# Layer 1 of a four-layer kernel: background pieces in two parts, linked convolution groups, and a preparation that waits for PSUM

## Chip, cores and metric

The kernel runs on one core of one Trainium2 chip, in float32 throughout. The metric is the device time of one execution in microseconds (us). A core has TensorE (PE, matrix multiplies into PSUM), VectorE (DVE), ScalarE (ACT), GpSimd (POOL), and DMA queues; the SyncE queue (SP) issues most loads. Each engine executes its own list of instructions in the order in which the program issues them.

## What is computed

The input is 8 images of 64 channels by 64 x 64 positions, and four layers follow each other. The change concerns layer 1 alone, a state space layer with a gated feed-forward part. Cut to what matters:

```python
xn = ln(x);  xm, z = split(xn @ in_proj)          # 64 -> 2 x 128 channels
u  = silu(conv3x3_depthwise(xm))                  # 128 channels, 4096 positions
for way in range(4):                              # rows, columns, and both backwards
    dt, B, C = project(u)                         # dt = softplus(...), 16 states
    h[n] = exp(dt * A[n]) * h[n] + dt * B[n] * u  # a scan over 4096 positions
    y += sum over n of h[n] * C[n]   (+ D * u)
x1 = x + out_proj(ln(y) * silu(z))
a, b = split(conv3x3_depthwise(conv1x1(ln(x1))))  # 2 x 170 channels
out = x1 + conv1x1(gelu(a) * b)
```

## The kernel before

**Steps and slots.** Layer 1 (function `layer1`) cuts each image's scan into 16 steps: four ways times four pieces of T = 1024 positions, so 8 images give 128 steps. A step is 16 slots, one for each of the 16 states. The function `stream` (which layers 2 and 3 use too) issues the slots one after another. In slot i it issues:

- SP: loads of B for state i+5 and of C for state i+3, each spread from one row to 128 partitions;
- POOL: `multiply_b(i+2)` (L465), hb = du * B, into one of three buffers;
- DVE: `scan(i)` (L481), which turns the decay dA and hb into h;
- DVE or POOL: `multiply_c(i)` (L495), h * C. In slots 1, 4, 7, 10 and 13 ("shared") POOL does it, in the next slot, and h gets a tile of its own in SBUF. In the other 11 slots DVE does it, and h overwrites the decay in PSUM;
- ACT: `keep` (L1211), one column of h for the next piece, and `decay(i+2)` (L472), the exponential for two slots later. The decays have two PSUM tiles;
- PE: `gather(i-2)`, which adds hc to the sum of the step in PSUM through the identity matrix (L287, four matrix passes). The first gather of a step stands in slot 2, and there the sum of the step before is drained (L1226 on ACT for the first way of an image, L1228 on DVE for the others).

**Background work.** Two kinds of work are threaded through the slots as Python generators (`Task`). One is `prepare` of the next step: a projection (L287 into `mm`), a copy to `dbl` (L1184), two small transfers (L1187), the matmul for dt (L1191), then softplus (L396) and du (L1198). The other is a queue named `behind` with, for each image, `finish` (norm of y, output projection), `begin` (norm, convolution and z of the image after the next) and `feed` (the feed-forward part). Inside them `statistics` computes means of squares (Square L907, mean L912, copy L917, small transfer L918, square root L922, reciprocal L924), `place` writes a normed tile into a padded image (ACT L895, POOL L896), `group` is one convolution group of 6 full-height (L879) and 6 half-height (L887) matmuls, and `gated` has three groups in each of four chunks (gelu L1091 and L1102, products L1094 and L1105). `finish` multiplies the norm by z on POOL (L1023) and then by the centred y on DVE (L1028).

**What sets the order.** All background work shares one PSUM tile, `mm`. A generator says at each `yield` what its next piece needs: True means that it holds `mm` and must go on before another may use it (`stream` keeps it in `held`), False that its next piece needs no PSUM, None that it is about to take `mm`, and CALM that it holds `mm` but goes on only in slots where neither this nor the next state is shared. In each slot `stream` advances the preparation by one piece and the background by one piece. A piece is issued before the slot's scan, and, where slot i-2 was shared, before its gather (`late`); after the scan come `multiply_c` and `decay(i+2)`. At slot 2 of each step (`start = 2`) the next preparation starts, and because it needs `mm`, this loop first issues everything that is held, at once:

```python
while self.held or self.urgent:
    self.advance(behind)
work = Task(steps[at + 1].prepare())
```

After the last slot `rest` finishes the last image's `finish` and `feed` with a second PSUM tile.

Of the kernel before, what the change touches and what calls it, by code (L numbers as in the profile page):

```python
# [13 lines left out]
PSUM = bass.MemoryType.PSUM  # L14
# [8 lines left out]
T = 1024  # L23
# [188 lines left out]
    return ap.rearrange("p (a b) -> p a b", b=ref.shape[2])  # L212


CALM, CALM_FREE = "calm", "calm, no PSUM"


class Task:

    def __init__(self, pieces):
        self.pieces, self.said, self.calm, self.over = pieces, None, False, False

    def step(self):
        try:
            self.said = next(self.pieces)
        except StopIteration:
            self.said, self.over = False, True  # L230
        self.calm = self.said in (CALM, CALM_FREE)
        if self.calm:
            self.said = self.said == CALM

# [15 lines left out]
class Net:  # L250
# [147 lines left out]
    def advance(self, behind, room=True, calm=True):  # L398


        while True:
# [9 lines left out]
                return  # L411
            queue.popleft()

    def stream(self, pools, ahead, steps, behind, rest=None):

# [49 lines left out]
        def decay(i):  # L467
            if i < total:
                s, n = steps[i // NS], i % NS
                dA[i] = pe.tile([128, T], F32, name="dA")  # L470
                for cut, A in s.lanes:
                    nc.scalar.activation(dA[i][:, cut], s.dt[:, cut], AF.Exp, scale=A[:, n : n + 1])  # L472
# [13 lines left out]
        def calm(i):  # L486

            return i + 1 >= total or not (shared(i) or shared(i + 1))
# [27 lines left out]
            multiply_b(i)  # L516
        for i in range(2):
            decay(i)
        work, self.held, self.urgent = None, None, deque()
        for i in range(total + 2):  # L520
            at, n = divmod(i, NS)
            need(i + ahead[0], "bc")
            need(i + ahead[1], "du")
            fetch(i + ahead[0])
            fetch_c(i + ahead[2])
            multiply_b(i + ahead[1])
            if 0 < i <= total and shared(i - 1):
                multiply_c(i - 1)


            first = i > NS and n == 2
            late = i > 1 and not first and steps[0].late and shared(i - 2)
            if i > 1 and not late and not first:
                gather(i - 2)
            if at + 1 < len(steps) and n == steps[at].start:
                steps[at + 1].ready()
                while self.held or self.urgent:
                    self.advance(behind)
                work = Task(steps[at + 1].prepare())
            if work is not None and not (self.held and work.said is None) and (calm(i) or not work.calm):  # L540
                work.step()
                if work.over:
                    work = None
            room = work is None or work.said is not True and (n < steps[0].early or hasattr(steps[at + 1], "du"))
            self.advance(behind, room, calm(i))
            if late:
                gather(i - 2)
            if i < total:
                scan(i)
            if first:  # L550
                gather(i - 2)
            if i < total:
                if not shared(i):
                    multiply_c(i)
            decay(i + 2)
        steps[-1].drain(acc.pop(len(steps) - 1))
        steps[-1].done()
        while self.held:
# [262 lines left out]
    def layer1(self, src, dst):  # L821
        nc, tc, d = self.nc, self.tc, self.d
        mid = self.hbm["x1a"]
        with ExitStack() as ctx:
# [65 lines left out]

            def place(rows, normed, g, b):

                yield False
                o = rows[:C, :, 1 : 1 + HW]
                nc.scalar.activation(o, like(normed[:C], o), AF.Identity, bias=b[:C], scale=g[:C])  # L895
                nc.gpsimd.tensor_copy(rows[C:, :, 2 : 2 + HW], o)  # L896

            def statistics(hold, centred, halves, eps, chunks=range(4)):

                rs = p1.tile([128, 32], F32, name="rs")
                for c in chunks:
                    ps = yield from centred(c)
                    sq = tp.tile([128, T], F32, name="tmp")
                    nc.scalar.activation(sq, ps, AF.Square)  # L907
                    ps = pp.tile([128, T], F32, name="mm")
                    if halves:
                        for r in range(2):  # L910
                            at, o = slice(r * C, r * C + C), slice(r * 512, r * 512 + 512)
                            nc.tensor.matmul(ps[:1, o], mean[at, 0:1], sq[at, o], start=True, stop=True)  # L912
                    else:
                        self.mm(ps[:1], mean[:, 1:2], sq)
                    yield True
                    ms = tp.tile([1, T], F32, name="tmp")
                    nc.scalar.copy(ms, ps[:1])  # L917
                    nc.scalar.dma_start(rs[c * 32 : c * 32 + 32, :], ms.rearrange("o (p e) -> o p e", e=32))  # L918
                yield False
                yield False  # L920
                rs = rs[chunks[0] * 32 : chunks[-1] * 32 + 32]
                nc.scalar.activation(rs, rs, AF.Sqrt, bias=eps[: len(chunks) * 32])  # L922
                yield False
                nc.vector.reciprocal(rs, rs)  # L924
                yield False
                if chunks[0] == 0:
                    hold["rs"] = h1.tile([1, L], F32, name="rs")
                row = hold["rs"][:, chunks[0] * T : chunks[-1] * T + T]
                nc.sync.dma_start(row.rearrange("o (p e) -> (o p) e", e=32), rs)
                yield False  # L930
                yield False
# [6 lines left out]
            def begin(b):  # L938
# [15 lines left out]
                n = (HW + 2) * (HW + 2)  # L954
# [19 lines left out]
                    yield from place(pad[0][:, 1 + c * 16 : 17 + c * 16], inv, g1, b1)  # L974
                hold["u"] = p2.tile([128, L], F32, name="u")
                for c in range(4):
                    yield
                    ps = pp.tile([128, T], F32, name="mm")
                    for half in range(2):
                        conv_half(ps, taps, slice(0, 128), pad, c * 16, half)  # L980
                        yield True
                    conv_right(ps, taps, slice(0, 128), pad, c * 16)
                    yield True
                    yield True
                    nc.scalar.activation(hold["u"][:, c * T : c * T + T], ps, AF.Silu, bias=cb)
                for c in range(4):
                    yield
                    ps = pp.tile([128, T], F32, name="mm")
                    for r in range(2):
                        at, f = slice(r * C, r * C + C), 1 + c * 16 + r * 8  # L990
                        o = ps[:, r * 512 : r * 512 + 512].rearrange("p (a b) -> p a b", b=HW)
                        nc.tensor.matmul(
                            o, w_z[at], pad[0][at, f : f + 8, 1 + r : 1 + r + HW], start=True, stop=True
                        )
                    yield True
                    z = tp.tile([128, T], F32, name="tmp")
                    nc.scalar.activation(z, ps, AF.Silu)  # L997
                    nc.scalar.dma_start(hz[b, :, c * T : c * T + T], z)
# [51 lines left out]
            def feed(b, part=None):  # L1050
# [37 lines left out]
                def gated(c):  # L1088
                    ps = yield from group(c, slice(0, 128))
                    g = tp.tile([128, T], F32, name="tmp")  # L1090
                    nc.scalar.activation(g, ps, AF.Gelu)  # L1091
                    yield
                    ps = yield from group(c, slice(128, 256))
                    nc.vector.tensor_tensor(g, ps, g, ALU.mult)  # L1094
                    yield
                    x = tokens(mid, b, c)
                    ps = yield from group(c, slice(256, 362))

# [4 lines left out]
                    yield True  # L1103
                    yield True
                    nc.vector.tensor_tensor(h[:42], ps[C : C + 42], h[:42], ALU.mult)  # L1105
                    yield
                    ps = pp.tile([128, T], F32, name="mm")
                    self.mm(ps[:C], pout[:, 0, :], g, start=True, stop=False)
                    yield True
# [32 lines left out]
            behind = deque()  # L1142
# [19 lines left out]
            ways = (1, 3, 2, 0)  # L1162

            class Step:
                start, early, late = 2, 8, True
                shared = (1, 4, 7, 10, 13)
                shaped = staticmethod(lambda t: t)

# [8 lines left out]
                def prepare(self):  # L1177
# [7 lines left out]
                    self.bc = hp.tile([NS, 2, T], F32, name="bc")  # L1185
                    for m in range(2):
                        nc.scalar.dma_start(self.bc[:, m, :], dbl[4 + m * NS : 4 + m * NS + NS])  # L1187
                    pt = pp.tile([128, T], F32, name="mm")
                    for r in range(2):
                        at, o = slice(r * C, r * C + 4), slice(r * 512, r * 512 + 512)  # L1190
# [55 lines left out]
            with tc.manual_schedule():  # L1246
# [4 lines left out]
                steps = [Step(b, k, j) for b in range(NB) for k in ways for j in range(4)]  # L1251
# [227 lines left out]
    def l2_scan(self, hx, hy):  # L1479
        nc, tc, d = self.nc, self.tc, self.d  # L1480
        with ExitStack() as ctx:
# [34 lines left out]
            carries = {}  # L1516

            class Step:
                bc_shape, start, early, late = [128, 2, T], 1, 0, False
                shared = (1, 4, 7, 10, 13)  # L1520
                rev = False
                shaped = staticmethod(lambda t: t)
# [220 lines left out]
    def l3_stage(self, s, src, dst):  # L1743
# [5 lines left out]
        W, H = 512, 512 // HW  # L1749
        with ExitStack() as ctx:  # L1750
# [103 lines left out]
            behind = deque()  # L1854
# [1 line left out]
            images = {}  # L1856

            class Step:
                bc_shape, start, early, late = [128, 2, W], 1, 0, False
                first = staticmethod(lambda n: 0.0)  # L1860
                keep = staticmethod(lambda n, h: None)
                shaped = staticmethod(lambda t: t.rearrange("p (j t) -> p j t", j=2))
# [155 lines left out]
```

## Time and profile before

| | us |
|---|---|
| median of 3 runs (25488.44 to 25513.53) | 25492.16 |
| the profiled execution, its own time | 25501.22 |
| its span, first to last instruction | 25499.4 |
| layer 1's slots, first scan to last scan (1337 to 8673) | 7336 |
| a step of layer 1 without background work (4020.0 to 4072.1) | 52.1 |
| a step with convolution groups (3786.0 to 3846.3) | 60.3 |

The slots of layer 1 are 29% of the span. A step's length is read as the distance between the scans of its first slot and of the next step's first slot. The sum over the whole span, where DVE is busy 88% and POOL 86%, is an average over four layers; the steps of layer 1 are where the change acts, and in them the two lengths of the table differ by the time that background work adds.

### The profile page before, as it was taken

The numbers are of one execution on the slowest core, as the hardware profiler recorded it, in microseconds if no ns is written. First come the engines' busy times: TensorE is split into PE (matmuls) and PEld (weight loads), VectorE is DVE, ScalarE is ACT, GpSimd is POOL, SyncE is SP. The second block draws the span as 40 slices with busy tenths as digits, with TensorE's granted clock in tenths as the row PEclk, the third lists the DMA queues.
The fourth block names the chain that finished last, engine by engine and source line by source line (L and its number), as shares of the span: only waits on it lengthen the run. The fifth ranks groups of instructions, "written<-read, shape, count | busy, mean of one in ns | idle before, by whom it ended". The sixth has DMA issues, their size and how long they took to land. (4 is left out here: it accounts for less than half of the span.)

```text
span 25499.4 us, 193264 instructions
## 1 busy us (share of the span) xinstructions
PE 21439.3 (84%) x53146; PEld 8356.0 (33%) x53146; DVE 22515.7 (88%) x13020; ACT 14749.0 (58%) x18562; POOL 22003.6 (86%) x10679
## 2 busy tenths in 40 slices
PE   8777888888888888877888888888878888888888
PEld 5522333333333323322333333333333333333333
DVE  4379989999889679965999999999989999999999
ACT  4345555555555455512666666666666666666666
POOL 0089999999999669953999999999989999999999
PEclk9888999999999999988999999999989999999999
DMA  2289899898888668821555555555545555555554
GB/s 60 80 285 319 312 315 315 309 316 314 308 312 313 209 237 323 325 77 37 168 170 169 170 168 170 169 169 167 168 155 169 169 169 167 171 167 170 168 171 157
DMA packets 1772399, 5282.72 MB, mean 207 GB/s; under 512 B 536352, under 2 KB 542564, under 8 KB 1703472
## 3 DMA queue, kind: packets, MB, share of 16 engines
q1 hardware_dynamic: 1744176, 5207.00, 60.2%
q10 hardware_dynamic: 27136, 63.34, 0.8%
q8 instruction: 423, 6.93, 0.1%
q14 instruction: 664, 5.44, 0.1%
HBM read 5112.85 MB, written 156.11 MB: 207 GB/s over the span
## 5 line engine op out<-in xcount | busy, mean ns | idle before, releaser
L465 POOL TENSOR_TENSOR hb<-du,bc 128x1024 f32<-128x1024 f32 x4608 | 10746.9, 2356 | 495.0 <-DVE h L481 329.6
L287 PE MATMUL acc<-hc,ident 128*128 128x512 f32 x18816 | 8893.4, 614 | 87.3 <-DVE img L1228 56.7
L472 ACT ACTIVATE dA<-dt,w_A 128x512 f32<-128x512 f32 x8192 | 5662.7, 691 | 4115.1 <-DVE hc L495 3127.9
L481 DVE TENSOR_TENSOR_SCAN dA<-dA,hb 128x1024 f32<-128x1024 f32 x3384 | 7725.9, 2283 | 283.0 <-ACT dA L472 109.0
L287 PE MATMUL acc<-h,ident 128*128 128x512 f32 x7808 | 4552.5, 713 | 2373.9 <-POOL h L495 2373.7
L287 PEld LDWEIGHTS acc<-hc,ident 128*128 128x128 f32 x18816 | 3695.6, 200 | 5299.5 <-issue 4672.2
L465 POOL TENSOR_TENSOR hb<-du,b 128x1024 f32<-128x1024 f32 x2048 | 4880.6, 2415 | 489.4 <-DVE h L481 255.6
L495 DVE TENSOR_TENSOR hc<-dA,bc 128x1024 f32<-128x1024 f32 x3296 | 4034.5, 1224 | 261.1 <-issue 8.9
L472 ACT ACTIVATE dA<-dt,w_l_A 128x1024 f32<-128x1024 f32 x2560 | 2856.5, 1117 | 1183.2 <-DVE hc L495 757.6
L481 DVE TENSOR_TENSOR_SCAN dA<-dA,carry,hb 128x1024 f32<-128x1024 f32 x1320 | 3094.5, 2344 | 169.7 <-ACT carry L1211 109.1
L287 PEld LDWEIGHTS acc<-h,ident 128*128 128x128 f32 x7808 | 1544.6, 215 | 5032.0 <-POOL h L495 3170.5
L481 DVE TENSOR_TENSOR_SCAN h<-dA,hb 128x1024 f32<-128x1024 f32 x1352 | 3082.0, 2280 | 48.1 <-ACT dA L472 43.0
L495 POOL TENSOR_TENSOR h<-h,bc 128x1024 f32<-128x1024 f32 x1312 | 3088.9, 2354 | 14.2 <-DVE h L481 14.2
L495 DVE TENSOR_TENSOR hc<-dA,c 128x1024 f32<-128x1024 f32 x1408 | 1723.2, 1224 | 118.0 <-DMA c<-bc 6.5
L495 POOL TENSOR_TENSOR h<-h,c 128x1024 f32<-128x1024 f32 x640 | 1519.1, 2374 | 7.5 <-ACT carry L1211 7.1
L481 DVE TENSOR_TENSOR_SCAN h<-dA,carry,hb 128x1024 f32<-128x1024 f32 x600 | 1404.7, 2341 | 82.4 <-ACT dA L472 79.2
L472 ACT ACT_TABLE_LOAD x1122 | 1439.5, 1283 | 21.3 <-ACT tmp L997 1.2
L1211 ACT COPY carry<-dA 128x1 f32<-128x1 f32 x1056 | 167.8, 159 | 1725.3 <-DVE hc L495 1662.7
L1885 PE MATMUL mm<-xn,taps 128*128 128x512 f32 x2048 | 937.7, 600 | 33.5 <-POOL xn L1851 31.3
L694 POOL MEMSET xf<- 128x24 f32 x33 | 4.3, 141 | 910.6 <-PE ps L715 701.9
L339 POOL COPY strip<-plain 64x1024 f32<-64x1024 f32 x256 | 266.3, 1040 | 462.2 <-ACT plain L1612 454.1
L1900 PE MATMUL mm<-u,w_xp 128*36 128x512 f32 x1024 | 516.6, 629 | 140.8 <-ACT u L1897 136.3
(310 smaller groups left out, 19000.0 us busy)
## 6 DMA issues: line engine op xcount, KB each, us to landing
bc<-bc SPq DMA_DIRECT2D x4096, 512.0 KB
b<-bc SPq DMA_DIRECT2D x2048, 512.0 KB
c<-bc SPq DMA_DIRECT2D x2048, 512.0 KB
bc<-bc SPq DMA_DIRECT2D x512, 1024.0 KB
tmp<-rs SPq DMA_DIRECT2D x93, 512.0 KB
raw<-x SPq DMA_DIRECT2D x64, 512.0 KB
inv<-rs SPq DMA_DIRECT2D x64, 512.0 KB
tmp<-x SPq DMA_DIRECT2D x192, 128.0 KB
```

What stands on the lines that cost most here:

```text
L287: self.nc.tensor.matmul(o, lhsT, r, start=start, stop=stop)
L339: self.nc.gpsimd.tensor_copy(pair[e][0][r * C : r * C + C, rows, 1 + r : 1 + r + HW], v)
L465: nc.gpsimd.tensor_tensor(s.shaped(hb[i]), s.shaped(s.du), B.pop(i), ALU.mult)
L472: nc.scalar.activation(dA[i][:, cut], s.dt[:, cut], AF.Exp, scale=A[:, n : n + 1])
L481: nc.vector.tensor_tensor_scan(h[:, way], dA[i][:, way], hb.pop(i)[:, way], s.first(n), ALU.mult, ALU.add)
L495: engine.tensor_tensor(s.shaped(o), s.shaped(h), CC.pop(i), ALU.mult)
L694: nc.gpsimd.memset(x[:, :, HW:], 0.0)
L1211: nc.scalar.copy(self.carry[:, n : n + 1], h[:, last : last + 1])
L1885: nc.tensor.matmul(tokens(px[:, j * W : j * W + W]), taps[k][:, m, j * 128 : j * 128 + 128], xn[:, :, f : f + HW], start=m == 0, stop=m == 1,)
L1900: nc.tensor.matmul(pd, xp[:, k, j, :], u[:, j * W : j * W + W], start=j == 0, stop=j == 1)
```

## The change

A piece may now come in two parts. A generator that says MID has its next piece issued in the same slot, after the slot's gather, scan, product and decay: the new function `complete`, called at the end of each slot, steps the preparation and the held task while they say MID. MID stands in `place` (before ACT and POOL write the tile), in `statistics` (before the mean), and in `prepare` (before the matmul for dt).

LINK stands where one convolution group, one z chunk or one gated product ends and the next begins. It is read as MID, so that the next group's first matmuls are issued in the same slot, unless a preparation is waiting for PSUM or is due in the next slot (`Task.wanted`); then it is read as None, as before.

A preparation that is due at slot 2 is now `pending`. It starts when nothing is held, and only from slot 2 + `patience` (4) on does it issue the held work at once. While it waits, no new background task takes `mm`. Layers 2 and 3 have `patience = 0`, no MID and no LINK. `statistics` says False once more before its square root.

```diff
-CALM, CALM_FREE = "calm", "calm, no PSUM"
+CALM, CALM_FREE, MID, LINK = "calm", "calm, no PSUM", "in two parts", "in two parts, or two pieces"
...
 class Task:
+    wanted = False
...
-        self.pieces, self.said, self.calm, self.over = pieces, None, False, False
+        self.pieces, self.said, self.calm, self.over, self.mid = pieces, None, False, False, False
...
-        self.calm = self.said in (CALM, CALM_FREE)
+        if self.said == LINK:
+            self.said = None if Task.wanted else MID
+        self.calm, self.mid = self.said in (CALM, CALM_FREE), self.said == MID
+        if self.mid:
+            self.said = True
...
+    def complete(self, work):
+        for task in (work, self.held[0] if self.held else None):
+            while task is not None and task.mid:
+                task.step()
+        if self.held and self.held[0].said is not True:
+            if self.held[0].over:
+                self.held.popleft()
+            self.held = None
...
             if at + 1 < len(steps) and n == steps[at].start:
                 steps[at + 1].ready()
+                pending = True
+
+            if pending and (n >= steps[at].start + steps[at].patience or not (self.held or self.urgent)):
                 while self.held or self.urgent:
                     self.advance(behind)
-                work = Task(steps[at + 1].prepare())
+                work, pending = Task(steps[at + 1].prepare()), False
...
+            Task.wanted = pending or n == steps[0].start - 1
             room = work is None or work.said is not True and (n < steps[0].early or hasattr(steps[at + 1], "du"))
-            self.advance(behind, room, calm(i))
+            self.advance(behind, room and not (pending and not (self.held or self.urgent)), calm(i))
...
             decay(i + 2)
+            self.complete(work)
...
@@ place
-                yield False
+                yield MID
                 o = rows[:C, :, 1 : 1 + HW]
                 nc.scalar.activation(o, like(normed[:C], o), AF.Identity, bias=b[:C], scale=g[:C])
...
@@ statistics
                     nc.scalar.activation(sq, ps, AF.Square)
+                    yield MID
                     ps = pp.tile([128, T], F32, name="mm")
...
+                yield False
                 yield False
                 yield False
                 rs = rs[chunks[0] * 32 : chunks[-1] * 32 + 32]
...
@@ begin
-                    yield
+                    yield LINK if c else None
                     ps = pp.tile([128, T], F32, name="mm")
...
-                    yield
+                    yield LINK
                     ps = pp.tile([128, T], F32, name="mm")
...
@@ gated (at three places)
-                    yield
+                    yield LINK
...
@@ Step
-                start, early, late = 2, 8, True
+                start, early, late, patience = 2, 8, True, 4
...
                         nc.scalar.dma_start(self.bc[:, m, :], dbl[4 + m * NS : 4 + m * NS + NS])
+                    yield MID
                     pt = pp.tile([128, T], F32, name="mm")
```

More of the change, by code (lines that the diff above doesn't have):

```diff
@@ L518, in stream @@
             decay(i)
-        work, self.held, self.urgent = None, None, deque()
+        work, pending, self.held, self.urgent = None, False, None, deque()
         for i in range(total + 2):
@@ L1091, in gated @@
                     nc.scalar.activation(g, ps, AF.Gelu)
-                    yield
+                    yield LINK
                     ps = yield from group(c, slice(128, 256))
                     nc.vector.tensor_tensor(g, ps, g, ALU.mult)
-                    yield
+                    yield LINK
                     x = tokens(mid, b, c)
@@ L1105, in gated @@
                     nc.vector.tensor_tensor(h[:42], ps[C : C + 42], h[:42], ALU.mult)
-                    yield
+                    yield LINK
                     ps = pp.tile([128, T], F32, name="mm")
@@ L1518, in l2_scan @@
             class Step:
-                bc_shape, start, early, late = [128, 2, T], 1, 0, False
+                bc_shape, start, early, late, patience = [128, 2, T], 1, 0, False, 0
                 shared = (1, 4, 7, 10, 13)
@@ L1858, in l3_stage @@
             class Step:
-                bc_shape, start, early, late = [128, 2, W], 1, 0, False
+                bc_shape, start, early, late, patience = [128, 2, W], 1, 0, False, 0
                 first = staticmethod(lambda n: 0.0)
```

## The prediction

> **What bounds the kernel now.** I read the busy time by stages first, for two steps of layer 1: one without background work, one with convolution groups (columns: window, length, then busy us of PE, PEld, DVE, ACT, POOL, then clock, DMA share, GB/s).
>
> ```profile
> 4020.01:4072.13 52.12, 38.13 (x73) 14.43 (x72) 50.71 (x29) 22.68 (x21) 50.10 (x23) 0.87 0.92 309
> 3785.96:3846.27 60.31, 53.66 (x137) 20.05 (x136) 53.18 (x31) 30.73 (x28) 51.63 (x23) 1.00 0.85 295
> ```
>
> In the first DVE and POOL are both full: 52.1 us is the floor of a step. In the second DVE works 2.5 us more, yet the step lasts 8.2 us more, so DVE stands still. Next, who DVE waits for in all of layer 1 (total us, times, longest):
>
> ```profile
> DVE dA L481 <- ACT carry L1211: 176.2, 133, 3.1
> ...
> DVE tmp L1105 <- ACT tmp L1102: 69.7, 13, 5.4
> DVE tmp L1028 <- POOL tmp L1023: 62.4, 27, 4.3
> DVE dA L481 <- ACT dA L472: 58.0, 47, 3.6
> DVE tmp L1094 <- PE mm L887: 56.3, 28, 6.6
> DVE h L481 <- ACT dA L472: 56.2, 30, 4.5
> ```
>
> Then DVE's timeline, once at a step's slot 2 and once at slot 4 (start, us, instruction, idle before):
>
> ```profile
> 3789.54 2.34 DVE L481 TENSOR_TENSOR_SCAN h<-dA,carry,hb 128x1024 f32<-128x1024 f32 x1
> 3798.09 1.22 DVE L1094 TENSOR_TENSOR tmp<-mm,tmp 128x1024 f32<-128x1024 f32 x1 [6.21 <-PE mm L887]
> ...
> 3979.63 2.34 DVE L481 TENSOR_TENSOR_SCAN h<-dA,carry,hb 128x1024 f32<-128x1024 f32 x1
> 3983.22 2.36 DVE L481 TENSOR_TENSOR_SCAN dA<-dA,carry,hb 128x1024 f32<-128x1024 f32 x1 [1.25 <-ACT carry L1211]
> ```
>
> and ACT's beside the second:
>
> ```profile
> 3982.00 1.12 ACT L472 ACTIVATE dA<-dt,w_l_A 128x1024 f32<-128x1024 f32 x1 [2.10 <-DVE h L481]
> 3983.06 0.17 ACT L1211 COPY carry<-h 128x1 f32<-128x1 f32 x1
> ```
>
> The first is the forced burst: a whole convolution group is issued in slot 2 to free `mm`, and DVE waits 6.2 us for it. The second I call a crossed decay: the decay of state 5 got the PSUM tile that scan 4 was still reading, not the one that was already free, so scan 5 waits for scan 4, then for an exponential.
>
> From the scan starts I took every slot's length, less the floor (3.5 to 3.6 us unshared, 2.25 to 2.3 shared, plus DVE's own extra instructions). The 7336 us of layer 1 hold 618 us of DVE standing still: crossed decays 223 (160 times), bursts at slot 2 112 (19), slots 3 and 4 where a preparation meets forced background work 89 (26), waits of L1028 for POOL 68, slot 2 to 3 41, the rest 85.
>
> **What the Trainium skill says.** "PSUM — Partial Sum Buffer", Engine vs sequencer instructions: ACT, DVE and POOL are strict FIFO, and matmuls start in program order, so a piece that waits holds up all behind it. The trace agrees: 6.2 us above. The same page, PSUM bank collisions: two engines need a dependency when they touch one bank, reads too. The trace agrees: ACT's read of dA waits for DVE's read of it (`carry` after `hc`, 1662.7 us of idle ACT). "ScalarE: Activation LUTs", What ACT_TABLE_LOAD costs: 1283 ns and a drain of 1380 ns. The trace has 1283 ns, and the next instruction starts 0.01 us later, so I use 1.28. "Perfetto Trace Analysis", Optimization Strategy: regular bubbles can mean too few buffers; here `mm` is one tile, and the decays have two.
>
> **The change, part by part.** I use the instruction order of both built programs and the durations above; all sums are against the profiled execution, 25501 us. Layers 2 and 3 keep their order and waits, so all happens in layer 1.
>
> *Waiting for PSUM.* The bursts go: 112 us. In the new order the preparation finds `mm` free at slot 2 in half of the steps, and starts at slots 4 to 6 in the others. It then meets no forced matmuls and copies: of the 89 us at slots 3 and 4 I take 65, of the 41 at slot 2 to 3 I take 18. A later preparation costs nothing while du comes before slot 14, which needs it (multiply_b is two ahead); in the new order it comes at slot 12 at the latest. B's rows are needed by SP at slot 11 and are written at slot 7, 12 us ahead. If that cover failed, SP would stop with every load behind it, but five states are loaded ahead (17 us).
>
> *Crossed decays.* Which PSUM tile a decay takes follows from the order. Counting decays that wait for the scan of the slot before gives 160 in the old order and 106 in the new. A shared slot followed by one lasts 3.60 us, else 2.26 (medians), 1.34 more; a few of those left will coincide with other waits, so I take 1.30: 54 fewer, 70 us.
>
> *Links.* A group is 12 full-height passes at 0.43 us and 12 half-height ones, two at a time, at 0.215: 7.8 us of PE, by the starts in PE's timeline. It took five slots and now takes four. A slot has 3.3 us, of which four gather passes take 1.72. Four slots offer 13.2 us, gathers and group need 14.7. Two or three groups in a row leave PE 5 to 7 us behind. The three products in `hcp` cover about four slots, but the drain at slot 2 (L1228) waits for the last gather, and L1094 for the last group: I take 10 us for each of 7 `feed`s, less what such waits cost now (about 0.7): +65. Bounds: 15, if the buffers absorb all but the drains, and 140, if half of the overdraft reaches DVE each time.
>
> z is worse. Its four chunks and the last silu fall into five slots in a row (13, 14, 15, 0, 1). Each costs ACT a table load, 1.03, 0.34 for the transfer, a table load back, a carry of 0.16 and a decay of 1.12: 5.2 us, together 26 against 15.2 us of DVE. With 2 us of lead DVE loses 8.5; the spread-out z loses about 2.3 now, so 6 more, in 7 `begin`s: +42 (bounds 5 and 80; in the stretch with z, 3608 to 3667, DMA is at 0.98, which could slow z's stores too).
>
> *Two parts.* The mean's and dt's matmuls move behind the gather in late slots only, so PE no longer waits there for `dbl` (74.7 us of idle PE at L1191, which DVE hardly feels): 0. `place` keeps ACT's order, but on POOL the copy now stands before `multiply_b` of the next slot, not behind it: it waits for ACT up to 3.5 us longer, with hb and the POOL product queued behind it. hb is ready 1 to 6 us ahead of its scan. Taking 4 of 8 copies per image at 0.3 us: +8 (bounds -15, because ACT's L1070 waits 56.7 us for these copies now, and +40).
>
> *L1028.* POOL's L1023 waits for z's load (46.6 us in 22 waits). The distance from load to use is the same in three chunks of four, but one slot pattern is 1.25 us shorter, and in one chunk du stands before L1023: +22 (bounds 0 and 50).
>
> *The end.* At the last scan the new order has one reciprocal more to go, of a tail of 190 us (8673 to 8861): +6 (bounds 0 and 20).
>
> Sum: -112 - 65 - 18 - 70 + 65 + 42 + 8 + 22 + 6 = -122. That gives 25379 us for the profiled execution, 9 us above the median shown, so 25370.
>
> **Rivals.** (a) *The links are nearly free*, costs at their lower bounds (15 + 5 - 15 + 0 + 0 = 5): -260, 25232. For it: the old steps with two groups already kept PE busy for 54 of 60 us without waits outside the bursts. Against it: z's sum on ACT. (b) *The burst is only spread out*: it was the same PE work, and PE overfilled by links gives it back at the drains: +140 for the groups, +80 for z, others as above: -9, 25483, no change. (c) *Slower, by ACT and PE in lockstep*: a linked group's first matmul waits for the gelu or silu that empties `mm`, in the same slot, and the next gather stands behind it on PE; ACT in turn has a table load before the next decay. Some 14 links in an image make 98 in seven. Against 265 us gained by the waiting part and the decays, links and the 36 us of other costs break even at 2.3 us a link; at 3.2 us it is 314 + 36 - 265 = +85, 25577. For it: ACT's decay is directly ahead of a scan; against it: a group's table loads (2.6 us) existed before, and ACT is busy 31 of 60 us. (d) *DMA takes the gain*: it runs at 0.92 in the free step. But that step ran at its floor, so DMA allows 52 us a step and I ask for 56; 3 in 100, a time near (b).
>
> **How the numbers follow.** Forecast 0.50 (25370, own range 25310 to 25440); (a) 0.17; (b) and (d) 0.18; (c) 0.15. The range 25240 to 25530 leaves out the far half of (a) and most of (c). About 0.2% (51 us) is what a measurement of this kernel can tell from no change. Faster by more: 0.70 (forecast, (a) and a little of (b)); within: 0.17; slower: 0.13.
>
> **What would show it.** In the trace after: no wait above 5 us of L1094 or L1105 at slot 2; DVE's wait for `carry` down by some 60 us; a stretch of about five slots with z in which DVE waits for ACT 8 us; waits of L1228 for PE, now 7.5 us in all, up to 20 to 60. Steps with groups near 57 us instead of 60, and no free step left in images 1 to 6. I am wrong if groups' steps stay at 60, or if L1094, L1228 and L1105 together wait as long as now (134 us).

## The result and the profile after

| | us | against before, 95% interval |
|---|---|---|
| before, median of 12 runs | 25495.83 | |
| after, median of 12 runs | 25498.62 | 1.0001 (0.9992 to 1.001) |
| span before, span after | 25499.4, 25505.3 | |
| layer 1, first scan to last scan, before and after | 7335.7, 7326.5 | |
| layer 1's last scan to layer 2's first, before and after | 484.2, 499.3 | |

The change makes no difference that can be measured; 25370 was forecast. Layers 2 and 3 are unchanged: from layer 2's first scan to the end, 16342.5 us before and 16341.9 after. In the kernel after, the lines have moved: the matmul helper L287 is L295, scan L481 is L500, hb L465 is L484, decay L472 is L491, softplus L396 is L404, carry L1211 is L1238, drain L1228 is L1255, the product of `finish` L1028 is L1054 (its POOL partner L1023 is L1049), a group's last matmuls L887 are L911, the gated products L1094 and L1105 are L1120 and L1131, `dbl` L1184 is L1210, and in `place` ACT's L895 is L919 and the copy L896 is L920.

The waits of DVE in layer 1 of the kernel after (total us, times, longest), to be held against those shown of before:

```profile
DVE dA L500 <- POOL hb L484: 124.0, 78, 65.5
DVE dA L500 <- ACT dA L491: 120.4, 77, 8.8
DVE dA L500 <- ACT carry L1238: 98.3, 82, 3.1
DVE tmp L1054 <- POOL tmp L1049: 64.4, 29, 3.5
DVE img L1255 <- PE acc L295: 57.1, 34, 3.9
DVE tmp L1120 <- PE mm L911: 48.7, 21, 3.7
DVE h L500 <- ACT carry L1238: 46.9, 15, 3.9
```

Two rows of before that the forecast did not show:

```profile
DVE dA L481 <- POOL hb L465: 79.8, 26, 65.5
...
DVE img L1228 <- PE acc L287: 5.5, 3, 2.8
```

What was meant to go has gone: the 69.7 us of L1105 are out of the list, and `dA` waits for `carry` 78 us less. Other rows have grown as much: the drain from 5.5 to 57.1 us (7.5 before in the forecast, which counts 10 us more), the scan into `dA` for the decay from 58.0 to 120.4, the scan into `h` for `carry` from 3.2 to 46.9, and the scan for POOL's hb from 79.8 us in 26 waits to 124.0 us in 78 (one wait of 65 us is in both). The last of these rows was hardly noticed in my forecast, and it turns out to be the most telling.

Where it went is seen best by slot. From the scan starts I again took each slot's length less its floor (my reckoning, us in all of layer 1):

| DVE stands still in slot | 1 | 2 | 3 | 4 | 6 and 7 | 13 to 15 and 0 | others | sum |
|---|---|---|---|---|---|---|---|---|
| before | 164 | 36 | 73 | 135 | 19 | 79 | 112 | 618 |
| after | 21 | 161 | 2 | 78 | 106 | 135 | 106 | 609 |

Slots 1, 3 and 4 give up 271 us. Slot 2 takes 125 back, slots 6 and 7 (the later preparations) 87, the slots around a step's end (z, gated products) 56. In slot 2 DVE now waits for the last gather before the drain and, at L1054, for POOL (57 and 53 us).

Steps with groups, after (columns: window, length, busy us of PE, PEld, DVE, ACT, POOL, then clock, DMA share, GB/s):

```profile
3781.44:3841.42 59.98, 55.08 (x137) 21.01 (x136) 53.30 (x32) 29.78 (x29) 55.90 (x25) 0.97 0.89 326
...
3724.34:3781.44 57.10, 50.44 (x125) 20.09 (x124) 53.37 (x31) 29.57 (x41) 52.99 (x23) 0.97 0.90 305
3841.42:3893.93 52.51, 47.60 (x115) 17.51 (x114) 51.05 (x30) 27.94 (x39) 47.31 (x21) 0.97 0.92 322
```

The steps are filled as the change wants it: the third, almost at the floor, holds 115 matmuls where the free step before held 73. But in the first POOL is busy longer than DVE (55.9 against 53.3 us) in a step that lasts 60.

### The profile page after: what moved, and what is told of

It is laid out like the page before. It is cut to its first block, busy times and chain, and to the rows that moved or that the text cites. A ratio compares the mean times of both kernels' runs of the same rounds, so it can differ in the third digit from the quotient of the medians.

```text
span 25505.3 us, 193250 instructions
## 1 busy us (share of the span) xinstructions
PE 21476.2 (84%) x53146; PEld 8359.0 (33%) x53146; DVE 22521.0 (88%) x13020; ACT 14743.4 (58%) x18560; POOL 22001.0 (86%) x10679
## 5 line engine op out<-in xcount | busy, mean ns | idle before, releaser
L484 POOL TENSOR_TENSOR hb<-du,bc 128x1024 f32<-128x1024 f32 x4608 | 10748.1, 2357 | 489.9 <-DVE h L500 334.1
L295 PE MATMUL acc<-hc,ident 128*128 128x512 f32 x18816 | 8913.8, 615 | 160.0 <-DVE img L1255 79.4
L491 ACT ACTIVATE dA<-dt,w_A 128x512 f32<-128x512 f32 x8192 | 5662.2, 691 | 4106.3 <-DVE hc L514 3127.5
L500 DVE TENSOR_TENSOR_SCAN dA<-dA,hb 128x1024 f32<-128x1024 f32 x3384 | 7724.9, 2283 | 264.6 <-ACT dA L491 116.4
L295 PE MATMUL acc<-h,ident 128*128 128x512 f32 x7808 | 4578.4, 716 | 2396.4 <-POOL h L514 2395.0
L295 PEld LDWEIGHTS acc<-hc,ident 128*128 128x128 f32 x18816 | 3668.4, 199 | 5398.6 <-issue 4642.3
L484 POOL TENSOR_TENSOR hb<-du,b 128x1024 f32<-128x1024 f32 x2048 | 4868.1, 2400 | 352.1 <-DVE h L500 208.4
L491 ACT ACTIVATE dA<-dt,w_l_A 128x1024 f32<-128x1024 f32 x2560 | 2856.8, 1117 | 1076.3 <-DVE hc L514 712.4
L500 DVE TENSOR_TENSOR_SCAN dA<-dA,carry,hb 128x1024 f32<-128x1024 f32 x1320 | 3094.3, 2344 | 223.1 <-ACT dA L491 82.0
L295 PEld LDWEIGHTS acc<-h,ident 128*128 128x128 f32 x7808 | 1574.9, 218 | 5081.6 <-POOL h L514 3234.7
L500 DVE TENSOR_TENSOR_SCAN h<-dA,hb 128x1024 f32<-128x1024 f32 x1352 | 3081.7, 2279 | 52.0 <-ACT dA L491 30.2
L500 DVE TENSOR_TENSOR_SCAN h<-dA,carry,hb 128x1024 f32<-128x1024 f32 x600 | 1404.0, 2340 | 104.7 <-ACT dA L491 73.9
L1238 ACT COPY carry<-dA 128x1 f32<-128x1 f32 x1056 | 167.6, 159 | 1612.5 <-DVE hc L514 1530.0
```

The lines of the kernel that those rows point to most:

```text
L295: self.nc.tensor.matmul(o, lhsT, r, start=start, stop=stop)
L484: nc.gpsimd.tensor_tensor(s.shaped(hb[i]), s.shaped(s.du), B.pop(i), ALU.mult)
L500: nc.vector.tensor_tensor_scan(h[:, way], dA[i][:, way], hb.pop(i)[:, way], s.first(n), ALU.mult, ALU.add)
L1238: nc.scalar.copy(self.carry[:, n : n + 1], h[:, last : last + 1])
```

## Experiments: which of the three parts

The first four kernels take the change apart: two parts (MID), links (LINK), waiting (patience).

```diff
@@ e1c_nowait (two parts and links)
-                start, early, late, patience = 2, 8, True, 4
+                start, early, late, patience = 2, 8, True, 0
@@ e2c_two_parts_only: that, and
-            self.said = None if Task.wanted else MID
+            self.said = None
@@ e3c_links_only: patience 0, LINK as in after, and
-                yield MID      # place; the MID of statistics and prepare removed
+                yield False
@@ e4c_waiting_only: patience 4, LINK None, MID as in e3c, and in rest()
+                for t in kept:
+                    t.run()
```

> The changed kernel with patience 0 in layer 1: the two-part pieces and the links stay, a preparation forces the held work at slot 2 as before. Theory A (the ledger of the two traces): the waiting removed about 204 us of standing DVE at slots 1 to 4, and paid 90 for late preparations and 42 at slot 2; of the decays 139 are crossed here instead of 106, 43 us more. So 204 - 90 - 42 + 43 = 115 us slower than the changed kernel, about 25610, ratio 1.004 to 1.005. Theory B (the background work costs the same wherever it is put): within 0.2% of the kernel before, 25450 to 25545.

> Only the pieces in two parts: no links, no waiting (157 crossed decays of 160). Theory A: the matmuls behind the gather were not what DVE waited for, so within 20 us of before but for the longer end, 25480 to 25515. Theory B: the same, 25450 to 25545. Should it be faster by over 50 us, the two parts are worth something that the later preparations ate.

> Only the links (150 crossed decays): the bursts at slot 2 stay. Theory A: the links cost the 38 us of the z chunks in a row and the 52 us at the gated products, less 13 us for decays: about 75 us slower than before, 25570. Theory B: within 0.2% of before, since the background then ends earlier and leaves free steps: 25450 to 25545.

> Only the waiting: no links, no two parts (86 crossed decays of 160). Some three chunks of the last feed are left over at the last scan and are issued after it, an estimated 100 us of tail by the 47 us that a chunk takes there less what overlaps. Theory A: -204 at slots 1 to 4, +90 late preparations, +42 at slot 2, -96 decays, +100 tail: 70 us faster than before, 25430, and in the slots alone 170 us. Theory B: the slots as before and the tail on top: 25590.

| | us | ratio to before | layer 1's slots, us | crossed decays |
|---|---|---|---|---|
| e1c: two parts and links | 25635.69 | 1.0057 (1.0042 to 1.0072) | 7480 | 139 |
| e2c: two parts | 25483.57 | 0.9996 (0.9987 to 1.0005) | 7321 | 157 |
| e3c: links | 25613.71 | 1.0047 (1.0032 to 1.0062) | 7449 | 150 |
| e4c: waiting | 25595.36 | 1.0040 (1.0025 to 1.0055) | 7300 | 86 |

Added to two parts, links cost 152 us (25484 to 25636); the waiting preparation then wins 137 back (25636 to 25499). Alone it can't be judged by its time: without links and two parts some three chunks of the last `feed` but one were left and ran after the last slot, so that the way to layer 2 took 624 us instead of 484. Its slots were 36 us shorter than before, with that work out of them. My ledger of standing times (theory A) missed here: e1c and e3c came out 26 and 44 us slower than it said, and e4c's slots 134 us longer.

By slot, e1c stands still 182 us in slot 1, 48 in slot 2, 70 in slot 3, 169 in slot 4 and 15 in slots 6 and 7. So the waiting preparation takes 320 us out of slots 1, 3 and 4, and puts 204 into slots 2, 6 and 7.

## Experiments: the later preparation

In the kernel after, ACT's copy `dbl` waits 160 us for PE's projection, which in the kernel before cost it 9. Three timelines of one step, PE, ACT and DVE, in the kernel after:

```profile
3261.66 1.98 PE L295 MATMUL acc<-hc,ident 128*128 128x512 f32 x4 [3.24 <-ACT img L1253]
3269.17 3.78 PE L295 MATMUL acc<-h,ident 128*128 128x512 f32 x4 [5.53 <-POOL h L514]
3272.75 2.48 PE L295 MATMUL acc<-hc,ident 128*128 128x512 f32 x4
3275.07 3.59 PE L295 MATMUL mm<-u,w_l_xp 128*68 128x512 f32 x4
```

```profile
3271.68 1.11 ACT L491 ACTIVATE dA<-dt,w_l_A 128x1024 f32<-128x1024 f32 x1
3278.69 1.01 ACT L1210 COPY dbl<-mm 68x1024 f32<-68x1024 f32 x1 [5.90 <-PE mm L295]
...
3280.56 0.16 ACT L1238 COPY carry<-dA 128x1 f32<-128x1 f32 x1 [0.86 <-ACT dbl L1210]
```

```profile
3277.51 1.22 DVE L514 TENSOR_TENSOR hc<-dA,c 128x1024 f32<-128x1024 f32 x1
3281.98 2.35 DVE L500 TENSOR_TENSOR_SCAN h<-dA,carry,hb 128x1024 f32<-128x1024 f32 x1 [3.24 <-ACT carry L1238]
```

The late projection stands on PE behind two gathers of its slot. `dbl` is reached by ACT first and holds up the carry and the decay behind it; DVE stands still 3.24 us. Two things can make PE late here: its order, or its clock, which had fallen. The Trainium skill, "TensorE: Matmul & The Clock Gate", What's actually happening, says that an idle window of 3413 ns brings the clock to half; the trace agrees: after 5.53 us of idle PE, four gather passes take 3.78 us instead of 1.98, and the granted clock from 3267.20 to 3273.90 is 0.50. Hence two experiments: extra gathers to keep PE warm, and a slot between the projection and `dbl`.

```diff
@@ e5_warm_pe: before the gather of state 0 (in slot 2), four steps of an image's first way, images 1 to 7
+                for _ in range(3):
+                    self.mm(acc[at], self.ident, o, start=True, stop=True)
@@ e6_xp_slot_ahead: in prepare, behind the projection
+                    if net.began > 2:
+                        yield True
@@ e9_xp_apart_late: that, and behind the dt matmul
-                    yield True
+                    if not net.began > 2:
+                        yield True
```

> The kernel after, but at slot 0 of those steps in images 1 to 7 that start a new image's way the gather's matmul is issued three more times (1.7 us of PE each, results overwritten by the real one), so that PE idles less at step starts. Theory 'half clock makes the late preparation's projection late': in those steps the waits of ACT's dbl copy for PE (160 us in all of layer 1 after) fall, and the standing still of DVE at late preparations (90 us) shrinks by a third or more: about 25460. Rival 'order alone': the projection stands behind a gather on PE whatever the clock, and the added PE work only delays gathers: 25500 to 25540. If the time stays within 20 us of 25498 and the half-clock time in layer 1 (1093 us) does not fall, the kernel has not tested the theory.

> The kernel after, but a preparation that began after slot 2 leaves one slot between its projection matmul and ACT's dbl copy (work left in the background queue at the end is issued after the last slot). Theory 'ACT reaches dbl before PE has done the projection, with the decays behind it': dbl's wait for PE falls from 160 us to under 30, the late preparations' 90 us of standing DVE to about 20, and layer 1's slots get some 50 us shorter (with 14 more crossed decays, +18); the preparation holds mm one slot longer, so background work is left for the end, up to 60 us of tail: 25450 to 25530 in all. Rival 'the late preparation's cost is in its other parts (decays of the slot, softplus, dt)': dbl's wait goes, but the 90 us stay within 20.

> The kernel after, but in preparations that begin after slot 2 the free slot behind the dt matmul is moved to between the projection matmul and ACT's dbl copy: mm is held as long as in the kernel after, and nothing is left over for the end. Theory 'a late preparation costs because dbl meets a PE that has not done the projection': dbl's wait for PE falls from 160 us to under 40, the standing still at late preparations from 90 us to about 25, layer 1's slots from 7326 to about 7270 and the end does not grow: about 25440 (30 more crossed decays are in it, some 10 us). Rival 'the slots of the earlier variant were shorter only because work was left for the end': slots stay within 15 us of 7326, 25490 to 25510. Rival 'the stall moves to softplus, which now follows the dt matmul at once': dbl's wait goes, softplus's wait for PE grows by as much, no gain.

| | us | ratio to before | slots | dbl waits | to layer 2 |
|---|---|---|---|---|---|
| e5: PE kept warm | 25527.52 | 1.0014 (1.0007 to 1.0021) | 7350 | 150 | 499 |
| e6: a slot ahead, mm held longer | 25526.24 | 1.0015 (1.0008 to 1.0022) | 7264 | 17 | 592 |
| e9: a slot ahead, mm held as long | 25492.74 | 1.0002 (0.9993 to 1.0010) | 7330 | 56 | 500 |

e5 does not decide between the two: it cut the half-clock time of layer 1 only from 1093 to 1001 us, and its extra passes are PE work ahead of the projection themselves, so `dbl`'s wait over all of layer 1 hardly moved. Single steps say more. In one preparation of each of images 1 to 7, e5 leaves no half clock in the 12 us before `dbl`, and `dbl` waits 3.1 to 4.1 us where it waited 4.9 to 6.0: some 2 us of such a wait go with the half clock, the larger part stays. It has a further cause, which I had not asked about. At full clock the projection's four passes take 3.59 us in the two ways that read columns and 1.88 to 1.94 us in the two that read rows, before and after alike, and all but 9 us of `dbl`'s waits lie in the column ways. There the projection and one gather fill PE for longer than a slot.

e6 looked like a confirmation: `dbl`'s wait goes and the slots are 62 us shorter. But the way to layer 2 is 93 us longer, by background work left for the end. e9 is the same cut without that loss, and it contradicts my reading: `dbl` waits 105 us less, and the slots are no shorter. Slot 6 does give up its 68 us, but slot 7 goes from 38 to 75, and 30 more decays are crossed. ACT's row in e9 shows the wait that is left, and softplus, now directly behind the dt matmul, waits 26.4 us for PE, which it did not before:

```profile
ACT dbl L1216 <- PE mm L295: 55.5, 24, 3.1
...
ACT L404 <- PE mm L1224: 26.4, 15, 3.5
```

## Experiments: crossed decays

A crossed decay shows some 1.25 us of standing DVE, and 54 fewer of them made 70 us of my sum. Their number in layer 1 can be set to zero with the order of instructions unchanged (layer 2 has pools of its own, so the 30 us that e7's expectation adds for it could not come about):

```diff
-pool("pe", 2, space=PSUM)
+(pool("pe0", 1, space=PSUM), pool("pe1", 1, space=PSUM))
...
-                dA[i] = pe.tile([128, T], F32, name="dA")
+                dA[i] = (pe[i % 2] if isinstance(pe, tuple) else pe).tile([128, T], F32, name="dA")
```

> The kernel before with the two PSUM tiles of the decays taken strictly in turn (even states one, odd states the other), so that no decay waits for the scan of the slot just before; nothing else moves. Theory 'each of 160 crossed decays in layer 1 costs 1.2 to 1.3 us': layer 1's slots 190 to 200 us shorter, 24 crossed decays of layer 2 some 30 us: 25490 - 220 = about 25270, ratio 0.991. Rival 'a crossed decay only shows the wait first; gated products, POOL's hb and the L1028 waits take its place': under 60 us gained, 25430 or more. My sum for the change took the first at full value (54 x 1.30).

> The changed kernel's two-part pieces alone (no links, no waiting preparation) with the decays' PSUM tiles taken in turn. If the gains add: 25484 - 220 = 25265, the best version so far, 10 us or less from the kernel before with the same decays. If pieces in two parts help only where a decay is late, this one is slower than that one by 10 us or more.

> The kernel after with the decays' two PSUM tiles taken strictly in turn: no decay waits for the scan of the slot before. At the price that the kernel before gave (160 crossed decays worth 46 us of slots, 0.29 each) 106 are worth 31 us: about 25470. At the price of my sum (1.30 each): 25360. If less than 10 us, a crossed decay costs nothing once steps are filled by links.

> Both: late preparations with a slot between projection and dbl, decays' tiles in turn. If the late preparations' wait is the reason why the waiting part did not pay, this is some 60 us under the kernel after with the tiles in turn, about 25410; if not, within 15 us of it.

> Pieces in two parts alone, no links, no waiting preparation, decays' tiles in turn (25434 so far), and in every preparation the free slot moved to between projection and dbl. There DVE stands still 136 us at slots 3 and 4, where the projection stands behind the forced work on PE and dbl waits for it. Theory: most of that goes, slots from 7250 to about 7180, 25370, the best version. Rival 'the forced work holds PE two slots and softplus then waits instead': within 15 us of 25434.

| | us | ratio to before | gained by the edit |
|---|---|---|---|
| e7: before, decays in turn | 25468.76 | 0.9993 (0.9984 to 1.0001) | 22 for 160 crossed |
| e8: two parts, decays in turn | 25433.99 | 0.9979 (0.9970 to 0.9987) | 50 for 157 |
| e10: after, decays in turn | 25452.27 | 0.9985 (0.9978 to 0.9992) | 46 for 106 |
| e11: e10 with e9's edit | 25428.16 | 0.9976 (0.9967 to 0.9985) | 24 more |
| e12: e8 with the projection a slot ahead in all preparations | 25451.11 | 0.9984 (0.9977 to 0.9991) | 17 lost |

The waits of DVE in e7:

```profile
DVE dA L481 <- ACT dA L472: 120.3, 89, 3.6
DVE dA L481 <- POOL hb L465: 102.8, 57, 65.3
...
DVE tmp L1094 <- PE mm L887: 71.6, 28, 6.6
```

The row `dA <- carry` is down from 176.2 us to 9.4, but a crossed decay is worth 0.14 us in the kernel before, 0.32 and 0.43 in the other two, and not 1.30. Compared slot by slot, the 160 slots themselves become 114 us shorter, not 200 (160 times 1.25): in many the next wait (a decay behind other ACT work, a product) ends almost as late. Six slots further, 55 of the 114 us are given back, over all slots 46 remain, and the end takes another 24. All three rows shown have grown, by 15 us or more (from 58.0, 79.8 and 56.3).

e11 shows that the later preparation is worth something once decays are uncrossed: 24 us, not the 90 that stood in the ledger. In e12 the same edit costs 17 us, where I had expected 64 of gain; that PE is busy over both slots where a burst was forced is my explanation, and not tested.

## Experiments: POOL's copy

One row is left: scans wait for hb 26 times before and 78 times after. POOL's queue at a copy of `place` in the kernel before, where the tile is ready when POOL comes to it:

```profile
3507.84 2.40 POOL L495 TENSOR_TENSOR h<-h,c 128x1024 f32<-128x1024 f32 x1
3510.30 1.03 POOL L896 COPY img<-img 64x1024 f32<-64x1024 f32 x1
3511.41 4.76 POOL L465 TENSOR_TENSOR hb<-du,b 128x1024 f32<-128x1024 f32 x2
```

and in the kernel after, then the DVE timeline of the kernel after:

```profile
3556.42 2.41 POOL L484 TENSOR_TENSOR hb<-du,b 128x1024 f32<-128x1024 f32 x1
3560.85 1.03 POOL L920 COPY img<-img 64x1024 f32<-64x1024 f32 x1 [2.02 <-ACT img L919]
3561.96 4.75 POOL L484 TENSOR_TENSOR hb<-du,b 128x1024 f32<-128x1024 f32 x2
3566.67 2.33 POOL L514 TENSOR_TENSOR h<-h,c 128x1024 f32<-128x1024 f32 x1
3568.97 4.72 POOL L484 TENSOR_TENSOR hb<-du,b 128x1024 f32<-128x1024 f32 x2
```

```profile
3564.39 2.36 DVE L500 TENSOR_TENSOR_SCAN dA<-dA,carry,hb 128x1024 f32<-128x1024 f32 x1 [0.17 <-POOL hb L484]
...
3571.38 2.36 DVE L500 TENSOR_TENSOR_SCAN dA<-dA,carry,hb 128x1024 f32<-128x1024 f32 x1 [1.06 <-POOL hb L484]
```

The copy waits 2.02 us for ACT, with hb behind it. POOL then works without a gap, and DVE pays most of it some 10 us later, at 3571.38. All copies of layer 1, what POOL stood idle for ahead of them, in the kernel before:

```profile
its engine sat idle before it (us, times) until:
  ACT carry L1211: 7.4, 6
  ACT strip L1069: 6.0, 6
```

and in the kernel after:

```profile
its engine sat idle before it (us, times) until:
  ACT img L919: 25.8, 18
  ACT strip L1095: 24.4, 14
  ACT strip L919: 22.3, 8
  ACT carry L1238: 1.6, 1
```

13 us have become 74. The other kernels show which part does it: with `place` as before it is 18 us with links (e3c), 1 with the waiting (e4c) and 14 with uncrossed decays (e7); with `place` in two parts it is 99 in e2c, 111 in e1c and 83 in e8. The test is to let ACT, which has just written the tile, copy it as well:

```diff
-                nc.gpsimd.tensor_copy(rows[C:, :, 2 : 2 + HW], o)
+                nc.scalar.copy(rows[C:, :, 2 : 2 + HW], o)
```

I first took POOL's load as a whole for the cause, and the expectations say so. (The second label is e11's kernel, unchanged.)

> The kernel before with the second half of a placed tile copied by ACT instead of POOL (57 copies of 1.04 us in layer 1's slots). Theory 'POOL is the next to be late, so what DVE no longer waits for is mostly not saved': here, where crossed decays and bursts still give POOL time, POOL's 59 us less are worth little: within 20 us of 25491. Rival 'ACT has no room, its copy delays the decays': slower by 20 us or more.

> The kernel after with the decays' tiles in turn and late preparations taken apart, unchanged: a second look beside its variant with ACT's copy, 25428 again within 15 us.

> The kernel after with the decays' tiles in turn, late preparations taken apart (25428), and the copy on ACT instead of POOL. DVE's waits for POOL's hb are most there (162 us, 122 times). Theory 'POOL is next': they fall to near 110 us and the time by 30 us or more, 25395. Rival 'POOL is not what takes the gain back (ACT, PE or DMA is)': within 15 us of 25428; rival 'ACT has no room': slower.

> The kernel after, only the placed tile's copy moved from POOL to ACT (57 x 1.04 us). If POOL is what kept the change from paying, this one is 20 to 50 us under the kernel after: 25450 to 25480. If POOL is next only where no decay is crossed, it stays within 15 us of 25498 (106 crossed decays give POOL its time), as the kernel before did (25492 against 25491).

> The kernel before with the decays' tiles in turn and the copy on ACT. The decays in turn alone gave 22 us (25469), the copy alone nothing (25492). If POOL is what took the rest of the decays' gain, both together give more than the sum: 25430 or less. If they add, 25469.

> Pieces in two parts alone (no links, no waiting preparation), decays' tiles in turn, the copy on ACT: against 25434 with the copy on POOL. If POOL is next there as well, 25400 or less. Against 25373 of the same with links and waiting: if this one is slower by 15 us or more, links and the waiting preparation pay once POOL and the decays make room; if not, they do not.

| copy on ACT in | copy on POOL, us | copy on ACT, us | ratio to before | gained |
|---|---|---|---|---|
| before (e13) | 25491.3 | 25491.97 | 0.9999 (0.9990 to 1.0007) | 0 |
| before, decays in turn (e17) | 25468.76 | 25467.86 | 0.9989 (0.9981 to 0.9998) | 1 |
| after (e16) | 25498.62 | 25421.29 | 0.9972 (0.9961 to 0.9983) | 77 |
| e11's kernel (e15) | 25428.16 | 25372.72 | 0.9954 (0.9939 to 0.9969) | 55 |
| two parts, decays in turn (e18) | 25433.99 | 25344.63 | 0.9941 (0.9924 to 0.9957) | 89 |

(e14, run beside e15, gave 25406.06 in its single run; against that e15 gains 33 us, so a gain between kernels run at different times can be off by some 20.) The line between the rows is clear. Where `place` is issued as before, ACT's copy gives nothing, with crossed decays or without, though the same 59 us of work leave POOL. Where `place` is in two parts, it gives 77 and 89 us in two kernels and 33 or 55 in the third. So e13 and e17 speak against "POOL's load is next", for which e15 and e16 alone seemed to speak, and 77 and 89 us are more than the load that left: what costs is the place of the copy in POOL's queue. DVE's waits for hb in layer 1, in e16 and then in e13:

```profile
DVE dA L500 <- POOL hb L484: 82.6, 26, 65.1
```

```profile
DVE dA L481 <- POOL hb L465: 81.4, 27, 65.4
```

In e16 the waits for hb are back at the 26 of the kernel before; in e13 they were never more. This row gives 41 of the 77 us. By my count to the last scan, some 29 more come at the drain, L1054 and L1120, which are not direct waits for hb. Undoing MID in `place` alone was not run; the two halves of `place` were separated only by moving the copy.

e18 is the best version: 25344.63 us, 0.6% under before, without links and without the waiting preparation. With both, and the projection a slot ahead, it is 25372.72 (e15). How much of these 28 us is that edit's, which cost e8 17, is not told apart.

## Why the prediction failed

The same edit on both sides gives the change's worth without POOL's copy: e13 to e16, 25491.97 to 25421.29, 71 us faster. With the copy on POOL it is 3 us slower. So the forecast's sign hung on one term, and its size on others too.

- *"`place` keeps ACT's order ... Taking 4 of 8 copies per image at 0.3 us: +8 (bounds -15 ... and +40)".* This step failed. The mechanism was named (the copy waits for ACT, with hb behind it), its size was not: 77 us, 1.4 for each of 57 copies, near twice the upper bound. I charged what DVE feels at once and trusted hb's lead of 1 to 6 us. But POOL is busy 92% of layer 1 (6774 of 7339 us after) and makes up little of a lost lead; the debt is paid slots later. One timeline above shows that; for the whole sum it is argued. No rival held it.
- *"54 fewer, 70 us."* This step failed as well. The count was right (106 crossed after). The price of 1.30 us was not: 0.14 to 0.43 in three removals, 8 to 23 us for 54.
- These two alone take some 115 to 130 us out of a sum of -122. That this closes the account is partly luck, since other terms were wrong too and cancel:
- *"A later preparation costs nothing while du comes before slot 14".* It did cost, through `dbl` ahead of the decays on ACT, not through du: 90 us in the ledger, 6 (e9) to 24 (e11) in time by the one remedy tried, which leaves a third of `dbl`'s wait.
- *"Waiting for PSUM": 112, 65 and 18.* The bursts went from slot 1 (164 to 21), yet slot 2 to 3 was to gain 18 and lost 125. I asked what goes and not what then ends last there: the drain for the last gather and L1054 for POOL. The part gained 137 us on top of the others, crossed decays included, where the forecast has 195 and 33 crossed decays.
- *"Links": 65 for groups, 42 for z.* The trace has 52 for gated products and 38 for z over before; five z slots in a row were to cost 8.5 us and cost 9.3. The drain at L1255 waits 57.1 us, within the 20 to 60 announced. As a part, links cost 118 us alone (e3c), near the forecast, and 152 on top of two parts, more than forecast.
- *"Two parts: 0".* As built they are worth 12 us (e2c), inside the noise. With the decays in turn and the copy on ACT they are worth 123 us (e17 to e18), which I had not foreseen. Which of their three places does it was not separated.
- *"L1028": +22.* It waits 64.4 us where it waited 62.4, so +2, inside the bounds.
- *"The end": +6.* 15, by scan starts.
- My sign of failure was 134 us of L1094, L1228 and L1105 together; they wait 106 us. It looked at DVE's partners in the changed pieces, and the loss came in by hb. Steps with groups are at 57.1 and at 60.0 us, where 57 was said.

Of the rivals, (b), the burst only spread out, gives the time measured. Its reason, PE overfilled by links, explains part of slot 2 and of the 152 us, but the copy on ACT wins 77 us with links as they are, so the time of (b) came about in another way. (d), DMA, did not hold the time: e18 moves the same data in 154 us less than the kernel after.

## What to carry to other kernels

When a piece is moved, go through every instruction in it by queue, and ask what stands behind one that will wait for another engine. Here POOL was busy 92% of layer 1 before and after: the same copy was harmless where its tile was ready and dear where hb had to wait behind it, though hb seemed to have a lead. Don't add up idle times as savings; take one such wait away whole and see what it is worth (here 46 us of slots for 200 us of crossed decays). And if a change moves nothing, look for a cheap edit that matters on one side of it only: the same copy was worth 0 us before and 77 after.

## What I had not expected

Moving 59 us of work off an engine that is busy 92% of a stage changed nothing in two kernels, and gave more than those 59 us in two others. In e13 the time set free went back into waiting: POOL's waits for DVE ahead of hb grew from 475 to 537 us. ACT paid little for it: its copy takes 1.05 us where POOL's takes 1.04, and in e13 the scans' wait for decays rose from 58.0 to 65.4 us.
